# A Mamba block beside a recurrence: elementwise steps moved from VectorE to GpSimd, gate results kept in PSUM, and a new order of the pieces

## The chip, the core and the metric

The kernel runs on one core of a Trainium2 chip. The core has five engines that run their own instruction streams and wait for each other by semaphores: TensorE (PE, matmuls into PSUM), VectorE (DVE, elementwise and scans), ScalarE (ACT, activations), GpSimd (POOL[...]) and SyncE (SP, which issues most DMAs). The metric is device time in microseconds of one execution; lower is better. All numbers are float32.

## What is computed

The input is x with 8 samples of 512 tokens and 256 features. Four layers follow, each with a normalized input and a residual:

```python
x = x + mamba_block(layernorm(x))       # layer 1
x = x + recurrence(layernorm(x))        # layer 2
x = x + attention(layernorm(x))         # layer 3
x = x + recurrence(layernorm(x))        # layer 4, the weights of layer 2
```

The Mamba block, cut to what matters here:

```python
h = layernorm(x, ln1_g, ln1_b)
xi, z = split(rmsnorm(h, rms_w) @ in_proj_w)
xc = silu(causal_conv4(xi) + conv_b)
dbc = xc @ x_proj_w
delta = softplus(dbc[..., :64] @ dt_proj_w + dt_proj_b)
Bm, Cm = dbc[..., 64:80], dbc[..., 80:96]
# for each of 256 channels and 16 states, over the 512 tokens:
hs = exp(delta * A) * hs_before + delta * xc * Bm
y = sum_over_states(hs * Cm) + D_param * xc
h = h + (y * silu(z)) @ out_proj_w
x = x + h
x = x + relu(layernorm(x, ln2_g, ln2_b) @ ffn_w1 + ffn_b1) @ ffn_w2 + ffn_b2
```

The recurrence goes over the 8 samples one after the other, with the 512 tokens as its batch:

```python
f = sigmoid(xt @ wf.T + c @ uf.T + bf)
i = sigmoid(xt @ wi.T + c @ ui.T + bi)
g = tanh(xt @ wc.T + c @ uc.T + bc)
c = f * c + i * g
# the output of all samples: tanh(x @ wo.T + c_final @ uo.T + bo)
```

## The kernel before

The program has two halves. In the first, `mamba_and_recurrence` (L769) runs layer 1 and, one sample behind it, layer 2's recurrence. In the second, `attention` (L1158) runs layer 3 with layer 4's recurrence in its gaps. The functions of the recurrence (`recurrent_step`, L560) serve both halves; `d.keep` is true in the second alone.

The first half is software-pipelined over the samples. Block b runs the scan of sample b in 16 slots. A slot has one `scan`: two units of 8 channels by 16 states on 128 partitions (32 units in all), a `tensor_tensor_scan` over 512 tokens for each (L381) and then a multiplication by C for each (L385). C lies in PSUM (copied there by `take_c`, L299). For a scan, ScalarE makes the decay `da` in PSUM (L365, three banks), GpSimd makes the increments `bx` in SBUF (L372, three buffers, two units at a time), and SP loads the rows of delta and delta*xc, repeated over the states, from DRAM into pairs of buffers (`load_unit`, L348, three pairs each). TensorE sums over the states every second slot (`y`, L388).

Around the scan, each slot runs pieces of other samples. The order is written out by hand in `SLOTS` (L713), `LAST` for block 7 (L733) and `REST` behind it (L752); `FRONT` (L761) runs ahead of block 0. Each engine runs its instructions exactly in the order of these words. The letter says whose piece it is: e is sample b+2 and i is sample b+1 (both of `mamba_in`, L168), a and c are sample b, o is sample b-1 (`mamba_out`, L403), r is sample b-1 and q sample b-2 (both of the recurrence). A name that ends in an underscore is the ScalarE part that evicts the matmul of the same name. `da0`, `da1`, `bx` and `ld` prepare units some slots ahead.

The pieces that the change and the prediction touch:

- `affine` (L183): h times ln1_g plus ln1_b, two VectorE instructions over 128 x 1024. `outer` and `residual` (L196, L200): u is x normalized, plus h.
- `soft_exp`, `soft_rest`, `soft_ln`, `soft` (L301 to L317): softplus of a number v with e = exp(-|v|) and w = 1 + e as relu(v) + ln(w) - ((w - 1) - e), where the last bracket is the rounding remainder of w. `soft` also makes delta*xc, after which `store_dl` and `store_dx` write both to DRAM for the next block's loads.
- `conv0`, `conv1` (L238), three VectorE steps each that read the in-projection's PSUM bank.
- `gate0`, `gate1` (L408): y plus D*xc, then times silu(z).
- `tanh` and `update` (L597, L605): the sigmoids are computed as (1 + tanh)/2 and the state is kept doubled, so the new state is half of (1 + f)*c plus (1 + i)*g. The three activations are read from the matmuls' PSUM banks and written to three SBUF tiles; the three VectorE steps of `update` then run in SBUF.

PSUM has eight banks here: three for da, one for C, one for y, and three (tag `mm`, `cx.fill`) for all other matmul results of the first half.

Of the kernel before, what the change touches and what calls it, by code (L numbers as in the profile page):

```python
# [167 lines left out]
def mamba_in(cx, a, t, b):  # L168
# [132 lines left out]
    def soft_exp():  # L301

        t.w = cx.tok.tile([P, KC, L], F32, tag="h", name=f"w_{n}")
        nc.scalar.activation(t.e, t.e, AF.Exp, scale=-1.0)
        nc.scalar.activation(t.w, t.e, AF.Identity, bias=cx.one)

    def soft_rest():
        nc.vector.scalar_tensor_tensor(t.e, t.w, -1.0, t.e, ALU.add, ALU.subtract)
        nc.vector.tensor_sub(t.dl, t.dl, t.e)
# [250 lines left out]
def recurrent_step(cx, d, b, tok, tok_tag, ch, ch_tag):  # L560
# [36 lines left out]
    def tanh(g, m):  # L597
        if g == 0:
            t.act = [
                cx.tmp.tile([P, L], F32, tag=f"act_{what}", name=f"act_{what}{m}_{n}")  # L600
                for what, _ in GATES
            ]
        gate_tanh(cx, g, m, t.ps[g, m], t.act[g])

    def update(m):  # L605
        if m == 0:
            t.s = cx.state.tile([P, KC, L], F32, tag="c", name=f"c_{n}")
        f, i, g = t.act
        for what, by in ((f, d.s[:, m, :]), (i, g)):
            nc.vector.scalar_tensor_tensor(what, what, 1.0, by, ALU.add, ALU.mult)  # L610
# [124 lines left out]
q.g0 bx ld da0 q.g0_ scan o.gate1 da1
q.f1 o.proj1 o.proj0 bx da0 y scan da1 o.add_proj ld o.stats
scan da0 o.norm bx o.turn1 o.turn1_ q.i1 ld da1 o.turn0
y ld q.update0 bx o.turn0_ o.up0 da0 da1 q.f1_ scan
da0 q.i1_ ld o.up1 da1 o.up0_ bx scan
ld y da0 bx scan da1  # L740
da0 bx o.up5 ld da1 scan o.up1_
da0 ld da1 y bx scan
o.up2 bx o.up3 o.up2_ scan ld da0 o.up3_ o.down1 c.gate0 o.down0 o.up4 da1 o.add1
o.up6 ld o.up4_ o.up5_ o.up6_ da0 scan y bx da1 o.up7
da0 ld o.add0 bx o.up7_ scan da1
scan bx o.residual o.down3 o.down2 c.bias o.add3 o.add2 y da0 q.output0 r.stats r.norm q.g1 ld da1
# [677 lines left out]
```

## Time and profile before

| | us |
|---|---|
| median of three runs | 1674.97 (1673.49 to 1677.93) |
| the profiled execution | 1674.03 |
| its span in the trace | 1672.3 |
| PE busy | 1483.9 (89%) |
| DVE busy | 1206.1 (72%) |
| ACT busy | 869.4 (52%) |
| POOL busy | 443.8 (27%) |

The page of the profile divides the span into 40 slices of about 42 us and gives each engine's busy share in tenths, 9 being 90% or more:

```profile
PE   3146888989898989898879999999999999999998
DVE  4499999999999998982136677567675766665435
ACT  4565767576766666442223555454554445454522
POOL 1346464655555555553100000000000000000000
```

The first 18 slices or so are layer 1 with layer 2's recurrence; attention begins at about 860 us. In a view of groups, a row gives the line of the code and the engine, the operation, output and inputs with shapes, the count, then the busy time and the mean duration of one in ns, and then how long the engine was idle just before them and who ended the wait. In the timeline a row gives the start and duration in us, and in brackets the idle time before it. A PE matmul in float32 leaves two records.

### The profile page before, as it was taken

How to read it: one execution, taken by the hardware profiler on the slowest of the kernel's cores; microseconds unless marked ns; L12 is line 12 of the kernel's file. 1: busy time of each engine (PE TensorE's matmuls, PEld its weight loads, DVE VectorE, ACT ScalarE, POOL GpSimd, SP SyncE). 2: the span in 40 equal slices, each digit the busy share in tenths (PEclk: the TensorE clock that was granted, in tenths of full speed). 3: DMA queues.
4: the chain of work that ended last, by engine and by line, in shares of the span. 5: the costliest groups of instructions: out<-in, count | busy, mean ns of one | idle time of the engine just before them, and what ended most of it. 6: DMA issues, size and time to landing. Idle time of an engine off the chain costs nothing.

```text
span 1672.3 us, 19586 instructions
## 1 busy us (share of the span) xinstructions
PE 1483.9 (89%) x6756; PEld 697.5 (42%) x6756; DVE 1206.1 (72%) x1678; ACT 869.4 (52%) x1315; POOL 443.8 (27%) x271
## 2 busy tenths in 40 slices
PE   3146888989898989898879999999999999999998
PEld 1012545555464646464642333333333333333346
DVE  4499999999999998982136677567675766665435
ACT  4565767576766666442223555454554445454522
POOL 1346464655555555553100000000000000000000
PEclk9576999999999999999986999999999999999999
DMA  5799888888788888860210111111011110100023
GB/s 190 193 237 240 216 226 210 246 207 239 197 228 218 220 204 221 224 150 26 66 51 20 26 35 30 34 24 39 15 40 24 38 27 26 24 9 26 27 94 126
DMA packets 110404, 196.03 MB, mean 117 GB/s; under 512 B 16448, under 2 KB 25984, under 8 KB 110304
## 3 DMA queue, kind: packets, MB, share of 16 engines
q1 hardware_dynamic: 107648, 186.61, 42.3%
q10 hardware_dynamic: 1824, 5.15, 0.9%
q0 software_dynamic: 832, 3.02, 0.6%
q8 instruction: 53, 0.87, 0.2%
q14 instruction: 47, 0.39, 0.1%
HBM read 159.06 MB, written 23.07 MB: 109 GB/s over the span
## 4 chain that ended last, share of the span: by engine, by line
PE 61%; DVE 21%; ACT 9%; issue 3%; DMA 3%; POOL 1%; SPq 1%; ACTq 0%; DVEq 0%; POOLq 0%
PE ps_s_c L998 10%; PE ps_e_c L998 9%; DVE hc_a L381 8%; PE ps_o_c L1044 8%; DVE hc_a L385 3%; PE ps_f_o L491 2%; ACT da_a L365 2%; PE ps_f_o L467 2%; PE ps_v_c L972 2%; PE ps_w_c L1085 2%; PE ps_f_d L540 2%; PE ps_i_d L540 2%; PE ps_g_d L540 2%; PE ps_f_d L549 2%; PE ps_i_b L540 2%
## 5 line engine op out<-in xcount | busy, mean ns | idle before, releaser
L1009 DVE TENSOR_REDUCE mp<-ps_s_c 128x2 f32<-128x1024 f32 x256 | 301.8, 1221 | 186.6 <-PE ps_s_c L998 186.1
L372 POOL TENSOR_TENSOR bx_a<-dx_rep_a,B_a 128x1024 f32<-128x1024 f32 x128 | 302.6, 2369 | 280.2 <-DVE hc_a L381 234.2
L1035 ACT ACTIVATE e_c<-ps_e_c 128x1024 f32<-128x1024 f32 x256 | 248.9, 1021 | 158.7 <-PE ps_e_c L998 155.8
L381 DVE TENSOR_TENSOR_SCAN hc_a<-da_a,bx_a 128x512 f32<-128x512 f32 x256 | 300.0, 1209 | 34.7 <-ACT da_a L365 21.8
L365 ACT ACTIVATE da_a<-dl_rep_a,neg_a 128x512 f32<-128x512 f32 x256 | 171.4, 684 | 85.9 <-DVE hc_a L381 65.2
L998 PE MATMUL ps_s_c<-keys,q_c 32*128 32x512 f32 x1024 | 186.9, 656 | 1.6 <-ACT e_c L1035 1.1
L998 PE MATMUL ps_e_c<-q_c,keys 32*128 32x512 f32 x1024 | 170.6, 650 | 3.7 <-DVE mp L1009 3.7
L385 DVE TENSOR_TENSOR hc_a<-hc_a,Cp_a 128x512 f32<-128x512 f32 x256 | 161.2, 671 | 0.0
L1044 PE MATMUL ps_o_c<-e_c,va 128*32 128x512 f32 x1024 | 139.8, 612 | 0.4 <-ACT oT_c L1060 0.3
L467 PE MATMUL ps_f_o<-h_o,w 128*128 128x256 f32 x512 | 124.3, 391 | 13.6 <-ACT f_o L480 5.9
L467 PEld LDWEIGHTS ps_f_o<-h_o,w 128*128 128x128 f32 x512 | 94.8, 192 | 57.4 <-ACT f_o L480 20.1
L491 PE MATMUL ps_f_o<-w,f_o 128*128 128x256 f32 x512 | 114.0, 381 | 0.0
L394 PE MATMUL y_a<-hc_a,sum 128*32 128x512 f32 x512 | 87.2, 654 | 22.8 <-DVE hc_a L385 12.8
L491 PEld LDWEIGHTS ps_f_o<-w,f_o 128*128 128x128 f32 x512 | 96.3, 190 | 15.7 <-ACT f_o L480 2.9
L998 PEld LDWEIGHTS ps_s_c<-keys,q_c 32*128 32x128 f32 x1024 | 60.5, 188 | 100.2 <-issue 39.6
L82 POOL TENSOR_TENSOR rs_d<-ve_d,neg_half 128x4 f32<-128x4 f32 x8 | 8.1, 1016 | 342.2 <-DVE ve_d L81 342.2
L998 PEld LDWEIGHTS ps_e_c<-q_c,keys 32*128 32x128 f32 x1024 | 51.8, 186 | 102.0 <-issue 67.3
L82 POOL TENSOR_TENSOR rs_c<-ve_c,neg_half 128x4 f32<-128x4 f32 x8 | 8.1, 1014 | 300.6 <-DVE ve_c L81 300.6
L480 ACT ACTIVATE f_o<-ps_f_o,vecs 128x256 f32<-128x256 f32 x128 | 52.5, 469 | 39.7 <-PE ps_f_o L467 39.5
L117 PE MATMUL ps_hT_a<-ident,h_a 128*128 128x128 f32 x64 | 12.9, 323 | 67.2 <-ACT h_a L206 60.7
L223 PE MATMUL ps_in_a<-hT_a,w_in 128*128 128x512 f32 x128 | 61.3, 615 | 0.8
L1044 PEld LDWEIGHTS ps_o_c<-e_c,va 128*32 128x32 f32 x1024 | 20.5, 108 | 93.2 <-issue 83.4
(213 smaller groups left out, 2091.2 us busy)
## 6 DMA issues: line engine op xcount, KB each, us to landing
dx_rep_a<-dx_dram_a SPq DMA_DIRECT2D x256, 256.0 KB, 5.7
dl_rep_a<-dl_dram_a SPq DMA_DIRECT2D x256, 256.0 KB, 5.6
x<-in_x_dram SPq DMA_DIRECT2D x8, 512.0 KB, 8.8
dl_dram_a<-dl_a SPq DMA_DIRECT2D x8, 512.0 KB, 4.7
dx_dram_a<-dx_a SPq DMA_DIRECT2D x8, 512.0 KB, 3.1
pre_dram_b<-pre_b ACTq DMA_DIRECT2D x8, 512.0 KB, 6.0
pre_back<-pre_dram_b SPq DMA_DIRECT2D x8, 512.0 KB, 3.4
keys<-xT_c SPq DMA_DIRECT2D x128, 32.0 KB, 1.9
```

Of the source, the lines that this page charges most:

```text
L365: cx.nc.scalar.activation(t.da[u], t.dl_rep[u // 2][:, u % 2, :], AF.Exp, scale=a.A[:, u : u + 1])
L372: cx.nc.gpsimd.tensor_mul(t.bx[pair], t.dx_rep[pair], t.B.unsqueeze(1).to_broadcast([P, 2, L]))
L381: cx.nc.vector.tensor_tensor_scan(t.hc[u], t.da[u], t.bx[pair][:, u % 2, :], 0.0, ALU.mult, ALU.add)
L385: cx.nc.vector.tensor_mul(t.hc[u], t.hc[u], t.Cp)
L394: cx.nc.tensor.matmul(t.y[k][head(j), :], a.sum[:, r, :], t.hc[4 * quad + j], start=(r == 0), stop=(r == QR - 1),)
L467: nc.tensor.matmul(ps[:, m, :], a.w1[:, k, ts(m0 + m, P)], t.h2[:, k, ts(half, L // 2)], start=(k == 0), stop=(k == KC - 1),)
L491: nc.tensor.matmul(ps, t.f[:, m, ts(c % 2, P)], a.w2[:, m, :], start=(m == 0), stop=(m == FC - 1),)
L540: cx.nc.tensor.matmul(ps, cx.gw[:, g, k, ts(m, P)], xT[:, k, :], start=(k == 0), stop=False)
L998: cx.nc.tensor.matmul(ps[:, i, :], lhs[rows, :], rhs[rows, :], start=True, stop=True)
L1009: cx.nc.vector.tensor_reduce(c.mp[:, t, h : h + 2, DH], ps, AX.X, ALU.max, negate=True)
L1035: cx.nc.scalar.activation(e, ps, AF.Exp)
L1044: cx.nc.tensor.matmul(po[head(j), :], c.va[b % 2][:, t, g * HG + j, :], es[j // 2][:, j % 2, :], start=(t == 0), stop=(t == TC - 1),)
```

## The change

For samples 1 to 7 the affine, the first residual and the two instructions of the softplus remainder run on GpSimd instead of VectorE (`side`). So that the remainder is a plain subtraction, ScalarE subtracts 1 from w in an instruction of its own, and the logarithm adds it again as its bias. In the first half, the tanh of gates f and g is written back to its own PSUM bank; a new piece `hold` makes (1 + f)*c into an SBUF tile and frees f's bank, and (1 + i)*g is written over g in PSUM. `gate_out` writes y plus D*xc back to y's bank. In the second half (`d.keep`) the same instructions as before are issued. The order of the pieces is new in `SLOTS` and `LAST`; `outer` and `residual` run two samples ahead instead of one. `LAST` follows `SLOTS` without the pieces of e and i.

```diff
@@ -170,6 +170,8 @@
     nc, v = cx.nc, cx.v
     n = f"a{b}"
 
+    side = nc.gpsimd if b else nc.vector
+
     def stats():
         t.x = cx.X[b]
@@ -181,8 +183,8 @@
         normalize(cx, t.h, t.x, t.inner)
 
     def affine():
-        nc.vector.tensor_mul(t.h, t.h, cx.rows3["ln1_g"])
-        nc.vector.tensor_add(t.h, t.h, cx.rows3["ln1_b"])
+        side.tensor_mul(t.h, t.h, cx.rows3["ln1_g"])
+        side.tensor_add(t.h, t.h, cx.rows3["ln1_b"])
 
     def square():
         t.ms = cx.small.tile([P, TC], F32, tag="ms", name=f"ms_{n}")
@@ -199,7 +201,7 @@
 
     def residual():
 
-        nc.vector.tensor_add(t.u, t.u, t.h)
+        side.tensor_add(t.u, t.u, t.h)
 
     def scale():
         for c in range(TC):
@@ -303,13 +305,14 @@
         t.w = cx.tok.tile([P, KC, L], F32, tag="h", name=f"w_{n}")
         nc.scalar.activation(t.e, t.e, AF.Exp, scale=-1.0)
         nc.scalar.activation(t.w, t.e, AF.Identity, bias=cx.one)
+        nc.scalar.activation(t.w, t.w, AF.Identity, bias=cx.minus)
 
     def soft_rest():
-        nc.vector.scalar_tensor_tensor(t.e, t.w, -1.0, t.e, ALU.add, ALU.subtract)
-        nc.vector.tensor_sub(t.dl, t.dl, t.e)
+        side.tensor_sub(t.e, t.w, t.e)
+        side.tensor_sub(t.dl, t.dl, t.e)
 
     def soft_ln():
-        nc.scalar.activation(t.w, t.w, AF.Ln)
+        nc.scalar.activation(t.w, t.w, AF.Ln, bias=cx.one)
 
     def soft():
         nc.vector.tensor_add(t.dl, t.dl, t.w)
@@ -408,9 +411,9 @@
     def gate_out(k):
 
         nc.vector.scalar_tensor_tensor(
-            t.xc[:, k, :], t.xc[:, k, :], v["D"][:, k : k + 1], t.y[k], ALU.mult, ALU.add
-        )
-        nc.vector.tensor_mul(t.zs[:, k, :], t.zs[:, k, :], t.xc[:, k, :])
+            t.y[k], t.xc[:, k, :], v["D"][:, k : k + 1], t.y[k], ALU.mult, ALU.add
+        )
+        nc.vector.tensor_mul(t.zs[:, k, :], t.zs[:, k, :], t.y[k])
 
     def proj(i):
@@ -563,7 +566,7 @@
     nc = cx.nc
     n = f"{d.name}{b}"
     t = Ctx()
-    t.ps = {}
+    t.ps, t.act = {}, {}
 
     def stats():
         t.x = cx.X[b]
@@ -595,20 +598,33 @@
         state(g, m)
 
     def tanh(g, m):
-        if g == 0:
-            t.act = [
-                cx.tmp.tile([P, L], F32, tag=f"act_{what}", name=f"act_{what}{m}_{n}")
-                for what, _ in GATES
-            ]
-        gate_tanh(cx, g, m, t.ps[g, m], t.act[g])
+
+        ps = t.ps[g, m]
+        if GATES[g][0] == "i" or d.keep:
+            t.act[g] = act_tile(g, m)
+        else:
+            t.act[g] = ps
+        gate_tanh(cx, g, m, ps, t.act[g])
+
+    def act_tile(g, m):
+        what = f"act_{GATES[g][0]}"
+        return cx.tmp.tile([P, L], F32, tag=what, name=f"{what}{m}_{n}")
+
+    def hold(m):
+
+        f = t.act[0]
+        t.held = f if d.keep else act_tile(0, m)
+        nc.vector.scalar_tensor_tensor(t.held, f, 1.0, d.s[:, m, :], ALU.add, ALU.mult)
 
     def update(m):
         if m == 0:
             t.s = cx.state.tile([P, KC, L], F32, tag="c", name=f"c_{n}")
-        f, i, g = t.act
-        for what, by in ((f, d.s[:, m, :]), (i, g)):
-            nc.vector.scalar_tensor_tensor(what, what, 1.0, by, ALU.add, ALU.mult)
-        nc.vector.scalar_tensor_tensor(t.s[:, m, :], f, 0.5, i, ALU.mult, ALU.add)
+        if d.keep:
+            hold(m)
+        i, g = t.act[1], t.act[2]
+        new = i if d.keep else g
+        nc.vector.scalar_tensor_tensor(new, i, 1.0, g, ALU.add, ALU.mult)
+        nc.vector.scalar_tensor_tensor(t.s[:, m, :], t.held, 0.5, new, ALU.mult, ALU.add)
         if m == KC - 1:
             d.s = t.s
@@ -635,8 +651,8 @@
 
     pieces = {f.__name__: f for f in (stats, norm)}
     for name, f in (
-        ("turn{}", turn), ("turn{}_", turn_), ("update{}", update), ("output{}", output),
-        ("output{}_", output_),
+        ("turn{}", turn), ("turn{}_", turn_), ("hold{}", hold), ("update{}", update),
+        ("output{}", output), ("output{}_", output_),
     ):
         for i in range(2):
             pieces[name.format(i)] = lambda f=f, i=i: f(i)
@@ -711,42 +727,42 @@
 
 
 SLOTS = """
-y da0 da1 a.take_c bx scan ld
-q.g0 i.outer bx ld da0 q.g0_ scan o.gate1 da1 i.rms i.residual
-i.scale q.f1 o.proj1 o.proj0 i.turn0 bx i.turn0_ da0 y scan da1 o.add_proj ld i.turn1 i.turn1_ o.stats
-i.proj0 scan da0 i.proj0_ o.norm i.conv0 bx i.proj1 o.turn1 i.proj1_ o.turn1_ q.i1 ld da1 o.turn0
-y ld q.update0 bx o.turn0_ i.conv1 o.up0 da0 da1 q.f1_ scan
-da0 i.proj2 q.i1_ i.proj3 ld i.silu_x o.up1 i.silu_z i.xproj da1 o.up0_ bx scan
-ld y da0 i.xproj_ bx scan da1
-da0 i.dt0 i.dt1 bx o.up5 e.stats ld i.dt0_ da1 scan i.dt1_ o.up1_ i.soft_exp
-da0 ld da1 y bx scan
-o.up2 bx o.up3 o.up2_ scan i.rows ld i.soft_rest da0 o.up3_ o.down1 c.gate0 o.down0 o.up4 da1 o.add1 i.soft_ln
-o.up6 ld e.center o.up4_ i.soft e.affine o.up5_ i.store_dx o.up6_ da0 scan y bx da1 o.up7
-da0 ld o.add0 bx o.up7_ scan e.square da1
-scan bx o.residual o.down3 o.down2 c.bias o.add3 o.add2 y da0 q.output0 r.stats i.store_dl r.norm q.g1 ld da1
-da0 q.output0_ scan bx da1 q.g1_ q.output1 r.turn0 ld r.turn0_
-scan q.update1 y r.turn1 ld bx r.turn1_ r.f0 da0 da1
-r.i0 bx da0 r.f0_ scan da1 ld q.output1_ r.i0_
+da0 y a.take_c bx i.rms i.scale scan q.g0 o.gate1 i.turn1 i.turn0 ld q.i0_ q.g0_ i.turn1_ da1 i.turn0_
+da0 scan q.update0 da1 ld o.proj0 o.proj1 i.proj0 bx
+scan bx y o.add_proj ld da0 i.proj0_ o.stats da1
+bx i.proj1 ld da0 q.f1 scan o.norm o.turn0 da1 i.proj1_
+ld o.turn1 i.conv0 o.turn0_ y i.proj2 o.turn1_ q.f1_ i.proj3 i.conv1 da0 da1 i.silu_x scan o.up0 bx q.hold1
+i.xproj o.up3 i.silu_z bx o.residual ld da0 scan da1
+i.xproj_ y bx o.up0_ e.stats da0 ld i.dt1 scan da1
+bx i.dt1_ da0 o.up1 o.up1_ q.i1 o.up2 e.center ld scan i.rows da1
+q.i1_ ld da0 o.up2_ da1 y scan bx i.dt0
+da0 o.up3_ i.dt0_ i.soft_exp bx o.down1 da1 o.down0 scan o.add1 ld
+ld scan e.outer i.soft_rest da0 o.up4 i.soft_ln o.add0 c.gate0 o.up5 y bx o.up7 o.up4_ da1 o.up6 o.up5_ e.affine o.up6_
+i.soft o.up7_ da0 da1 scan bx i.store_dx q.output0 o.down3 o.down2 o.add3 ld
+e.square scan da0 o.add2 da1 ld bx y
+da0 r.stats q.output0_ q.g1 q.output1 q.g1_ r.norm i.store_dl scan r.turn0 c.bias r.turn0_ bx r.turn1 da1 ld
+r.turn1_ q.update1 r.f0 e.residual da0 q.output1_ y r.f0_ da1 ld scan bx
+ld scan da0 da1 r.hold0 bx r.i0
 """.strip().split("\n")
...
@@ -754,15 +770,15 @@
 o.turn0 o.turn0_ o.turn1 o.turn1_ o.up0 o.up0_ o.up1 o.up1_ o.up2 o.up2_ o.up3 o.up3_ o.down0
 o.down1 o.add0 o.up4 o.up4_ o.up5 o.up5_ o.add1 o.up6 o.up6_ o.up7 o.up7_ o.down2 o.down3 o.add2
 o.add3 r.stats r.norm r.turn0 r.turn0_ r.turn1 r.turn1_
-r.f0 r.f0_ r.i0 r.i0_ r.g0 r.g0_ r.update0
-r.f1 r.f1_ r.i1 r.i1_ r.output0 r.output0_ r.g1 r.g1_ r.update1 r.output1 r.output1_
+r.f0 r.f0_ r.hold0 r.i0 r.i0_ r.g0 r.g0_ r.update0
+r.f1 r.f1_ r.hold1 r.i1 r.i1_ r.output0 r.output0_ r.g1 r.g1_ r.update1 r.output1 r.output1_
 """.strip().split("\n")
 
 FRONT = """
 i.stats e.stats i.center i.affine i.square i.outer i.rms i.residual i.scale i.turn0 i.turn0_
-i.turn1 i.turn1_ i.proj0 i.proj0_ i.proj1 i.proj1_ i.conv0 i.conv1 e.center i.proj2 i.proj3
+i.turn1 i.turn1_ i.proj0 i.proj0_ i.proj1 i.proj1_ i.conv0 i.conv1 e.center e.outer i.proj2 i.proj3
 i.silu_z i.silu_x i.xproj i.xproj_ e.affine i.dt0 i.dt0_ i.dt1 i.dt1_ i.rows i.soft_exp i.soft_rest
-i.soft_ln i.soft i.store_dl i.store_dx e.square
+i.soft_ln i.soft i.store_dl i.store_dx e.square e.residual
 """
@@ -1254,6 +1270,8 @@
     make_identity(nc, cx.ident)
     cx.one = const.tile([P, 1], F32, name="one")
     nc.gpsimd.memset(cx.one, 1.0)
+    cx.minus = const.tile([P, 1], F32, name="minus")
+    nc.gpsimd.memset(cx.minus, -1.0)
     cx.neg_half = const.tile([P, 2 * TC], F32, name="neg_half")
     nc.gpsimd.memset(cx.neg_half, -0.5)
```

More of the change, by code (lines that the diff above doesn't have):

```diff
@@ L730 @@
+ld scan e.outer i.soft_rest da0 o.up4 i.soft_ln o.add0 c.gate0 o.up5 y bx o.up7 o.up4_ da1 o.up6 o.up5_ e.affine o.up6_
[4 more added lines that the diff above has]
+ld scan da0 da1 r.hold0 bx r.i0
 """.strip().split("\n")
 LAST = """
-y da0 da1 a.take_c bx scan ld
@@ L735 @@
[L735 to L746, printed above, removed]
@@ L747 @@
-da0 q.output0_ scan bx da1 q.g1_ q.output1 r.turn0 r.turn0_
-scan q.update1 y r.turn1 r.turn1_ r.f0 da0
-r.i0 r.f0_ scan q.output1_ r.i0_ r.g0 r.g0_ r.update0 r.f1 r.f1_ r.i1 r.i1_ r.output0 r.output0_ r.g1 r.g1_ r.update1 r.output1 r.output1_
+da0 y a.take_c bx scan q.g0 o.gate1 ld q.i0_ q.g0_ da1
+da0 scan q.update0 da1 ld o.proj0 o.proj1 bx
+scan bx y o.add_proj ld da0 o.stats da1
+bx ld da0 q.f1 scan o.norm o.turn0 da1
+ld o.turn1 o.turn0_ y o.turn1_ q.f1_ da0 da1 scan o.up0 bx q.hold1
+o.up3 bx o.residual ld da0 scan da1
@@ new lines @@
+y bx o.up0_ da0 ld scan da1
+bx da0 o.up1 o.up1_ q.i1 o.up2 ld scan da1
+q.i1_ ld da0 o.up2_ da1 y scan bx
+da0 o.up3_ bx o.down1 da1 o.down0 scan o.add1 ld
+ld scan da0 o.up4 o.add0 c.gate0 o.up5 y bx o.up7 o.up4_ da1 o.up6 o.up5_ o.up6_
+o.up7_ da0 da1 scan bx q.output0 o.down3 o.down2 o.add3 ld
+scan da0 o.add2 da1 ld bx y
+da0 r.stats q.output0_ q.g1 q.output1 q.g1_ r.norm scan r.turn0 c.bias r.turn0_ bx r.turn1 da1
+r.turn1_ q.update1 r.f0 da0 q.output1_ y r.f0_ scan
+scan r.hold0 r.i0 r.i0_ r.g0 r.g0_ r.update0 r.f1 r.f1_ r.hold1 r.i1 r.i1_ r.output0 r.output0_ r.g1 r.g1_ r.update1 r.output1 r.output1_
```

## Prediction

> **What bounds the kernel now.** I began with the page's slices: DVE stands at nine tenths in the first half alone, so only the first half (0 to about 850 us) is touched by a lighter VectorE. Next I cut that half by sample, from one take_c (L299) to the next: blocks 0 to 7 begin at 55.3, 146.1, 228.5, 319.4, 408.5, 499.1, 588.5 and 677.3 us. Windows over four of them:
>
> ```profile
> core 0: us, PE busy (x) PEld busy (x) DVE busy (x) ACT busy (x) POOL busy (x), PEclk, DMA share, GB/s
> 146.10:228.50 82.40, 67.12 (x259) 39.34 (x258) 80.49 (x121) 55.83 (x98) 48.60 (x27) 0.88 0.88 226
> 319.40:408.50 89.10, 81.52 (x321) 46.90 (x320) 85.84 (x126) 60.82 (x108) 48.51 (x27) 0.98 0.85 224
> 588.50:677.30 88.80, 81.52 (x321) 47.03 (x320) 82.04 (x114) 56.97 (x96) 46.57 (x24) 0.98 0.85 216
> 677.30:775.00 97.70, 91.17 (x348) 52.74 (x347) 76.02 (x107) 41.11 (x73) 39.32 (x20) 0.97 0.57 143
> ```
>
> Read: in a steady block VectorE works 85.8 of 89.1 us, GpSimd little over half. But the third line is a natural experiment. Block 6 prepares no sample two ahead, so VectorE has 4 us less to do than in block 5 (82.0 for 86.0), and the block is only 0.6 us shorter than block 5's 89.4. The chain of waits in block 6 lies on TensorE from 632 to 660 us. So TensorE is a second bound close behind the first; block 7 is TensorE's altogether.
>
> The groups by form, and three places of the timeline:
>
> ```profile
> L308 DVE SCALAR_TENSOR_TENSOR e_a<-w_a,e_a 128x1024 f32<-128x1024 f32 x8 | 18.3, 2282 | 9.9 <-ACT w_a L305 9.9
> L309 DVE TENSOR_TENSOR dl_a<-dl_a,e_a 128x1024 f32<-128x1024 f32 x8 | 9.8, 1225 | 0.3
> L372 POOL TENSOR_TENSOR bx_a<-dx_rep_a,B_a 128x1024 f32<-128x1024 f32 x128 | 302.6, 2369 | 280.2 <-DVE hc_a L381 234.2 <-DMA dx_rep_a<-dx_dram_a 45.8 <-DMA dl_rep_a<-dl_dram_a 0.2
> ...
> 460.17 2.36 POOL L372 TENSOR_TENSOR bx_a<-dx_rep_a,B_a 128x1024 f32<-128x1024 f32 x1 [2.88 <-DVE hc_a L381]
> 461.19 2.42 DVE L308 SCALAR_TENSOR_TENSOR e_a<-w_a,e_a 128x1024 f32<-128x1024 f32 x1
> ...
> 694.65 5.11 POOL L372 TENSOR_TENSOR bx_a<-dx_rep_a,B_a 128x1024 f32<-128x1024 f32 x2
> 696.60 0.96 DVE L610 SCALAR_TENSOR_TENSOR act_f_b<-act_f_b,c_b 128x512 f32<-128x512 f32 x1
> 697.48 2.83 DVE L610 SCALAR_TENSOR_TENSOR act_i_b<-act_i_b,act_g_b 128x512 f32<-128x512 f32 x1
> ...
> 431.05 0.63 PE L117 MATMUL ps_h_o<-ident,un_o 128*128 128x128 f32 x4 [2.19 <-DVE xc_a L241]
> 432.55 3.78 PE L540 MATMUL ps_i_b<-xT_b,gw 128*128 128x512 f32 x4 [0.87 <-ACT h_o L452]
> 436.12 3.12 PE L549 MATMUL ps_i_b<-c_b,gw 128*128 128x512 f32 x4
> ```
>
> At 461.19 an instruction that costs 1.23 us elsewhere ends 1.2 us after GpSimd's does: it waited. At 696.60 two GpSimd instructions stand back to back; VectorE's f update gets in between them, its i update then waits for the second (2.83 instead of 0.68), and the pair of GpSimd instructions takes 5.11 instead of 4.68. The two engines take turns. The last lines show a TensorE that ran dry for 3 us and then needs 6.9 us for eight records that take 3.76 elsewhere (1.88 for four at 753.13).
>
> [...]
>
> **The change, part by part, for a steady block.**
>
> 1. *VectorE loses.* Affine L184 and L185 2.44, residual L202 1.22, L308 with its wait 2.42, L309 1.22. The two f updates took 1.90 and 1.05 us in this block (401.84 and 430.82)[...]: the 0.69 of the undisturbed ones, so 1.57 less. The gated sum i*g, and the D term written to PSUM, change by under 0.1 each. Together 8.9: 86.0 becomes 77.1 us.
>
> 2. *GpSimd gains* five instructions of 2.36, 11.8 us: 48.5 becomes 60.3 of some 87. In throughput covered. Its FIFO matters: the softplus pair stands behind bx 11, the affine between bx 12 and 13. I followed the stream: bx 13 is ready about 5 us before its scan, so the scans are not starved.
>
> 3. *ScalarE gains* one 1024-wide Identity (w - 1), 1.15 as L305: 62 of 87, covered, except where it delays part 4.
>
> 4. *What becomes late: soft (dl + w, then dl * xc).* In the new order soft_exp, soft_rest, soft_ln and soft stand in slots 9, 10, 10, 11 (before: 7, 9, 9, 10). ScalarE can't pass the decay of unit 21 before scan 18 is done, since da has three banks. From that moment S, at issue pitch: da 0.58, up's Relu pair 0.72, dt pair 1.16, Exp 0.97, two Identity 2.1, da 0.58, e.outer 2.0, da 0.58, table load 1.28, Ln 1.06: S + 11.0. VectorE arrives after scan 19, two multiplies, an add, scans 20 and 21 with multiplies, an add and the gate: S + 8.0. A stall of 3.0. At S + 11.0 GpSimd is inside bx 12 (softplus pair from S + 5.6 to 10.3, bx 12 to 12.7): 1.6 more[...]. After the add GpSimd takes its turn with the first affine, 2.36, before the multiply gets in. So 7 us in all. Bounds: 0 if ScalarE runs ahead of my walk[...], 9.4 if both instructions meet a whole one; I take 7.
>
> 5. *TensorE.* The work is unchanged: up 14.6, down 14.0, y 8.0, in 7.0, x and dt 3.6, gates 20.6, outputs 3.6, out_proj 3.6, transposes 3.3, each from back-to-back stretches, 78.3 us. Before, it waits and runs slowly for 10.5 more. In the new order f1 fills the wait for o.norm, but f1 keeps one of three banks until hold1 at the end of slot 4. Both o transposes use one bank with a ScalarE copy between them (0.8), in2 waits for the second conv (about 1.6), up0 for hold1 (0.5), and xproj is queued behind up0. I find 4 to 5 us of waits, and 3 to 4 of half clock if the gap in slots 3 and 4 triggers it as at 432 us: 83 to 87. I take 86 to 87; nothing below 78.3, and above by rival D.
>
> 6. *Moved pieces and DMA queues.* store_dx still follows soft; store_dl goes from slot 12 to 13 and lies two loads ahead of the first dl load that reads it, so SP waits some 3.5 us there (landing 4.7 on the page). The loads are needed about 5 us later than they then land: hidden. At 0.85 DMA share a block of 87 needs 0.87; block 1's 0.88 fed a VectorE that was 98% busy: no bound.
>
> 7. *FRONT.* e.outer (2.06, four L108) now precedes the Silu on ScalarE, and the second Identity (1.15) precedes soft_rest; the chain runs through ScalarE's L108, L252, L255, L304 and L305 there. Nothing hides either: +3.2.
>
> 8. *Block 7 and the rest.* TensorE-bound. f1 ahead of the transposes covers part of the 4.7 us idle at 690: -2 (0 to -5). REST's last update loses one of three steps, 0.6. The attention half keeps its operations (d.keep): 0.
>
> VectorE then needs 77.1 + 7 + 1 to 2 of ScalarE waits = 85 to 86, TensorE 86 to 87. I take 87 for blocks 2 to 5 (mean now 90.0): 4 x 3.0 = 12.0. Block 6: 88.8 to 86.5, 2.3. Block 1 has no f updates of the recurrence: 7.3 saved, 6.3 lost to soft, 1.0. Block 0: DVE-bound from 86 us on, 6.1 saved, 6 lost, 0. Sum: 12.0 + 2.3 + 1.0 + 2.0 + 0.6 - 3.2 = 14.7. The profiled execution took 1674.03 (span 1672.3 and 1.7 around it), within 1 of the median 1674.97: 1674.0 - 14.7 = **1659**.
>
> **Rivals.** A is the above; with the period between 85 and 89 it spans 1648 to 1669.
>
> B: ScalarE and GpSimd are early, soft doesn't stall[...]. Both engines then meet near 82.5. For it: GpSimd idle for 40 of 89 us. Against: da's three banks keep ScalarE in step. Gains 7.5 x 4, 6.3, 4, 2.6, less 3.2: 1634.
>
> C: the gains of blocks just pay for FRONT: period 89, within 5 us of 1674.
>
> D, slower: the held banks. With one of three banks kept from f1 to hold1, and from g to its update, TensorE's queue stands behind a VectorE instruction at the end of a slot, runs dry[...]. It decides once TensorE's waits and slow stretches exceed 11.7 us a block (78.3 + 11.7 = 90.0; 10.5 now). At 92 a block: 2 x 4 + 3.2 + 1.0 + 3.2 lost = 15: 1689. For it: block 6 shows TensorE close to the bound, and slot 4 has these waits in a row. Against: slots 0 to 3 give it filler.
>
> **The numbers.** A 0.42, B 0.20, C 0.13, D 0.25. About 0.3% (5 us) is what a measurement here can tell from no change: faster is A and B, 0.62; same C, 0.13; slower D, 0.25. The range goes from B's time to D's, 1634 to 1690; A's own is 1648 to 1669.
>
> **What would show it.** Right: the groups of soft (dl, then dx, on VectorE) with waits on ScalarE's w and means well above 1.22; hold at 0.69; take_c 86 to 88 us apart; the first scan 3 us later. Wrong: soft at 1.22 without waits (B); take_c over 90 apart with TensorE waiting for act_f or c_b (D); scans waiting for bx, which would refute part 2.

## The result, and the profile after

The changed kernel takes 1666.2 us (median of six runs, 1661.0 to 1668.3) against 1673.6 (six runs, 1673.2 to 1677.9): ratio 0.9947, 95% interval 0.9931 to 0.9964. It is faster, by half a percent. The profiled execution took 1665.1 with a span of 1663.3, so 9.0 us are to be found between the traces. Cut at the `take_c` copies (L301 now), the gain and the loss stand apart:

| stretch | before | after | gain | predicted |
|---|---|---|---|---|
| FRONT | 55.3 | 58.9 | -3.6 | -3.2 |
| blocks 0 and 1 | 90.8 + 82.4 | 93.0 + 83.7 | -3.5 | +1.0 |
| blocks 2 to 5, mean of one | 90.0 | 86.8 | 4 x 3.2 | 4 x 3.0 |
| block 6 | 88.8 | 86.1 | +2.7 | +2.3 |
| block 7 and all behind it | 995.0 | 994.6 | +0.4 | +2.6 |

Windows of the changed kernel over blocks 0, 1 and 3 (length, then busy time and count of each engine, granted clock, DMA share, GB/s):

```profile
58.90:151.90 93.00, 41.46 (x93) 10.11 (x94) 71.39 (x89) 47.62 (x75) 59.64 (x28) 0.59 0.91 229
151.90:235.60 83.70, 69.08 (x261) 40.43 (x260) 78.47 (x116) 58.89 (x102) 60.84 (x32) 0.87 0.93 229
323.30:409.40 86.10, 81.77 (x321) 47.18 (x320) 80.64 (x123) 63.00 (x108) 61.01 (x32) 0.98 0.91 230
```

The third line, a steady block: GpSimd 61.0, TensorE as before at 81.8, and VectorE 80.6 where the sum had 77.1. The groups by form of VectorE in that block say where the 3.5 are:

```profile
L320 DVE TENSOR_TENSOR dx_a<-dl_a,xc_a 128x1024 f32<-128x1024 f32 x1 | 3.3, 3266 | 0.0
L318 DVE TENSOR_TENSOR dl_a<-dl_a,w_a 128x1024 f32<-128x1024 f32 x1 | 2.6, 2582 | 1.8 <-ACT w_a L315 1.8
L617 DVE SCALAR_TENSOR_TENSOR act_f_b<-ps_f_b,c_b 128x512 f32<-128x512 f32 x3 | 2.1, 685 | 0.0
L504 DVE TENSOR_TENSOR x<-x,ps_f_o 128x256 f32<-128x256 f32 x4 | 1.7, 418 | 3.2 <-PE ps_f_o L494 3.2
```

The two steps of `soft` cost 1.22 each without a neighbour; here they take 2.58 and 3.27, so 3.4 us are spent waiting inside them, and 1.8 more ahead of them for the logarithm. A third wait, 3.2 us for TensorE ahead of an x addition, was not in the forecast. The timeline of the next block shows the turn-taking:

```profile
464.65 2.36 POOL L312 TENSOR_TENSOR dl_a<-dl_a,e_a 128x1024 f32<-128x1024 f32 x1
466.60 1.15 ACT L315 ACTIVATE w_a<-w_a,one 128x1024 f32<-128x1024 f32 x1
466.97 2.37 POOL L375 TENSOR_TENSOR bx_a<-dx_rep_a,B_a 128x1024 f32<-128x1024 f32 x1
467.83 2.59 DVE L318 TENSOR_TENSOR dl_a<-dl_a,w_a 128x1024 f32<-128x1024 f32 x1 [1.84 <-ACT w_a L315]
469.30 3.34 POOL L186 TENSOR_TENSOR h_a<-h_a,rows 128x1024 f32<-128x1024 f32 x1
470.46 3.26 DVE L320 TENSOR_TENSOR dx_a<-dl_a,xc_a 128x1024 f32<-128x1024 f32 x1
472.72 3.21 POOL L187 TENSOR_TENSOR h_a<-h_a,rows 128x1024 f32<-128x1024 f32 x1
```

The addition waits until bx ends at 469.3, then GpSimd waits for it (3.34 instead of 2.36), then the multiplication waits for GpSimd. That is the sequence which part 4 of the forecast walked through. But does it cost time? The chain of waits through that block, in order of time (start, length, what):

```profile
432.12 0.64 PE ps_h_o L117 x4
...
434.73 1.87 PE y_a L397 x8
436.60 3.79 PE ps_in_a L225 x8
...
456.74 3.66 PE ps_f_o L494 x16
...
460.77 1.23 DVE hc_a L384
...
462.71 2.00 ACT u_a L108 x4
...
466.60 1.16 ACT w_a L315
...
467.83 2.60 DVE dl_a L318
...
470.46 3.26 DVE dx_a L320
```

Not shown are VectorE's pieces on both sides: from the `take_c` at 409.4 to 432.0 and from 473.7 to the next `take_c` at 495.3 the chain is VectorE without a wait. So a block is one run of VectorE (scans, updates, statistics, convolution), then one of TensorE from the transposes on, then the softplus with ScalarE's part ahead of it. The chain shows one route only. The experiments ask how far behind it the next one is.

### The profile page after: what moved, and what is told of

Read it like the earlier page. It is cut to its first block, busy times and chain, and to the rows that moved or that the text cites. A ratio compares the mean times of both kernels' runs of the same rounds, so it can differ in the third digit from the quotient of the medians.

```text
span 1663.3 us, 19592 instructions
## 1 busy us (share of the span) xinstructions
PE 1487.2 (89%) x6756; PEld 700.3 (42%) x6756; DVE 1169.9 (70%) x1643; ACT 884.3 (53%) x1323; POOL 529.9 (32%) x307
## 4 chain that ended last, share of the span: by engine, by line
PE 67%; DVE 19%; ACT 5%; DMA 4%; issue 3%; POOL 2%; SPq 1%; DVEq 0%; ACTq 0%; POOLq 0%
PE ps_s_c L1014 10%; PE ps_e_c L1014 9%; DVE hc_a L384 8%; PE ps_o_c L1060 8%; PE ps_f_o L470 5%; PE ps_f_o L494 4%; DVE hc_a L388 3%; PE ps_in_a L225 2%; PE ps_v_c L988 2%; PE ps_w_c L1101 2%; PE ps_f_d L543 2%; PE ps_i_d L543 2%; PE ps_g_d L543 2%; PE ps_f_d L552 2%; PE y_a L397 2%
## 5 line engine op out<-in xcount | busy, mean ns | idle before, releaser
L397 PE MATMUL y_a<-hc_a,sum 128*32 128x512 f32 x512 | 92.0, 699 | 23.9 <-DVE hc_a L388 15.5
L225 PE MATMUL ps_in_a<-hT_a,w_in 128*128 128x512 f32 x128 | 68.1, 671 | 1.1 <-ACT hT_a L220 1.1
```

The lines of the kernel that those rows point to most:

```text
L225: nc.tensor.matmul(ps, a.in_proj[:, k, ts(m, P)], t.hT[:, k, :], start=(k == 0), stop=(k == KC - 1))
L397: cx.nc.tensor.matmul(t.y[k][head(j), :], a.sum[:, r, :], t.hc[4 * quad + j], start=(r == 0), stop=(r == QR - 1),)
```

## The experiments

All were timed in five rounds with the kernel before beside them, but for the two on the order, in three. The ratio is to the kernel before on the same chip, and a difference in us below is one of two ratios times 1673.6. The last column is the mean of blocks 2 to 5 in the profiled execution, one for each kernel. How far such a single trace can be trusted is seen in FRONT: its words are the same in eight of these kernels, and it took from 58.8 to 60.7 us.

| run | median, us | ratio to before (95%) | block, us |
|---|---|---|---|
| before | 1673.6 | 1 | 90.0 |
| the change | 1666.2 | 0.9947 (0.9931 to 0.9964) | 86.8 |
| e1 outer late | 1664.1 | 0.9939 (0.9926 to 0.9953) | 86.9 |
| e2 affine away | 1661.3 | 0.9917 (0.9900 to 0.9935) | 86.8 |
| e3 all on VectorE | 1692.3 | 1.0105 (1.0088 to 1.0121) | 92.5 |
| e4 gates in SBUF | 1689.2 | 1.0096 (1.0079 to 1.0114) | 91.0 |
| e5 conv early | 1672.1 | 0.9996 (0.9987 to 1.0004) | 87.7 |
| e6 FRONT and rms | 1660.7 | 0.9930 (0.9918 to 0.9943) | 86.8 |
| e7 old order | 1723.9 | 1.0308 (1.0291 to 1.0325) | 97.0 |
| e8 order alone | 1710.9 | 1.0225 (1.0208 to 1.0242) | 96.3 |
| e9 conv and norm early | 1660.1 | 0.9916 (0.9900 to 0.9933) | 85.5 |
| e10 both | 1654.5 | 0.9890 (0.9874 to 0.9907) | 85.4 |
| e11 spare work in the slack | 1665.0 | 0.9939 (0.9926 to 0.9952) | 86.8 |
| e12 the same work in VectorE's run | 1688.4 | 1.0094 (1.0077 to 1.0110) | 89.7 |

The steady blocks come in two lengths. In the change blocks 3 and 4 take 86.0 us, blocks 2 and 5 take 87.5. The trace of the change shows one stretch in each in which TensorE's granted clock was 0.50, behind the transposes of the o sample: 3.4 us long in the former (433.5 to 436.9 in block 4) and 6.8 in the latter (519.0 to 525.8 in block 5). In e1, e2 and e11 two of the four blocks took 86.0 to 86.1 us and two 87.3 to 88.0, and e6 has the same mean, so these means can be compared.

### e1 and e2: relieve the softplus

```diff
-ld scan e.outer i.soft_rest da0 o.up4 i.soft_ln o.add0 c.gate0 o.up5 y bx o.up7 o.up4_ da1 o.up6 o.up5_ e.affine o.up6_
+ld scan i.soft_rest da0 o.up4 i.soft_ln o.add0 c.gate0 o.up5 y bx o.up7 o.up4_ da1 o.up6 o.up5_ e.affine o.up6_
...
-e.square scan da0 o.add2 da1 ld bx y
+e.square e.outer scan da0 o.add2 da1 ld bx y
```

> e.outer (four Identities of ScalarE, 2.00 to 2.06 us, between the softplus's Exp and its Ln) is moved two slots down, behind e.square. Theory SOFT (part 4 of the forecast: the late softplus delays VectorE, and VectorE's delay ends the block): the Ln ends 2.06 us earlier, VectorE's wait for it goes from 1.8 us to 0 in blocks 2 to 6 and from about 4.0 to 1.9 in blocks 0 and 1; 5 x 1.8 + 2 x 2.06 = 13 us less than the changed kernel, some 1653 us, steady blocks 84 to 84.5 us. Theory TENSORE (part 5: TensorE's queue with its waits and slow stretches sets some 86 us, the softplus's stall lies in its shade): within 2 us of 1666, with another wait of VectorE in the place of the one removed.

For e2 only `e.affine` moves, from the end of slot 10 to slot 9 behind bx:

```diff
-da0 o.up3_ i.dt0_ i.soft_exp bx o.down1 da1 o.down0 scan o.add1 ld
+da0 o.up3_ i.dt0_ i.soft_exp bx e.affine o.down1 da1 o.down0 scan o.add1 ld
```

> GpSimd's affine is moved from behind the softplus's remainder to slot 9, into GpSimd's idle 7 us before the remainder. Theory SOFT: the multiplication of dl and xc on VectorE falls from 3.26 us to about 1.2 since no GpSimd operation takes turns with it (that of dl and w keeps its 2.6 because of bx), 2.0 us a block in seven blocks, some 14 us less: 1652 us, and the wait for the Ln stays at 1.8. Theory TENSORE: within 2 us of 1666. If GpSimd is the limit in blocks 0 and 1 (bx late behind remainder and affine), these two shorten by more than the 2.0.

Neither shortened a steady block. In e2 the multiplication still took 3.26 us: with the affine gone, GpSimd's next instruction in the order of the words is a bx, which could take the turn; that it did was not shown. The expectation had overlooked that another instruction stands next in the queue. e2's median is some 5 us under the change's, and the intervals hardly overlap; but its trace shows equal blocks, and that execution, at 1664.9, was the slowest of its four. Whether the place of the affine is worth some us stays open. In e1 the wait for the logarithm did go, and a wait of 1.0 us for GpSimd's remainder (L312) came, with the addition at 3.37 instead of 2.58: 0.8 us saved by one, 0.8 lost by the other. So neither run made the softplus as a whole shorter. What e1 shows is the chain of its block 3, at the place where the softplus stood:

```profile
370.30 7.10 PE ps_f_o L494 x32
377.40 3.45 PE ps_f_o L470 x16
380.86 1.00 PE y_a L397 x8
381.85 3.65 PE ps_f_o L470 x16
385.50 1.73 PE ps_o_b L636 x8
387.23 3.47 PE ps_f_o L494 x16
390.72 0.04 DVE x L504
```

TensorE runs on without a gap through the whole of that stretch, and the x addition in slot 11 needs its result. It starts 67.85 us after `take_c` (322.87); in the changed kernel VectorE came through the softplus to the same addition at 477.17, 67.78 us after 409.39, and TensorE's 16th record for it ended at 477.13 in the same trace. The two routes are a tie within 0.1 us. The softplus's stall is real, but a shorter one could not have started this addition earlier as long as TensorE's run is as long as it is. That is read from the two traces; no run took the stall away.

### e11 and e12: the same spare work at two places

Six statistics instructions whose result nobody reads, ahead of the x addition in slot 9 (e11) or ahead of the scan in slot 13 (e12):

```diff
+    def spare():
+        st = cx.small.tile([P, 6], F32, tag="spare", bufs=1, name=f"spare_{n}")
+        for c in range(6):
+            nc.vector.bn_stats(st, t.x[:, c % TC, :])
...
-da0 o.up3_ i.dt0_ i.soft_exp bx o.down1 da1 o.down0 scan o.add1 ld
+da0 o.up3_ i.dt0_ i.soft_exp bx o.down1 da1 o.down0 scan i.spare o.add1 ld
```

> Six statistics operations (128x256, 0.41 us each, 2.5 us) of VectorE whose result nobody reads are added ahead of the first x addition in slot 9, where VectorE of the changed kernel waits 3.1 us for TensorE and 1.8 us for the Ln. HANDOVER: they fill slack that TensorE's run covers; blocks stay at 86 to 87, within 4 us of 1666. BUSY of VectorE (its 80.6 us plus waits set the block): 7 x 2.5 = 17 us more, 1683.

> The same six statistics operations of VectorE (2.5 us) at another place: in slot 13, ahead of a scan, inside VectorE's own run from the last x additions to the transposes. HANDOVER: all of it is on the path, 2.5 us a block in seven blocks, 17 us more than 1666: 1680 to 1686, steady blocks 88.5. BUSY of TensorE: within 3 us of 1666, as at the other place.

Block 3 of e11, the window and VectorE's waits in it (all waits, how many, the longest):

```profile
323.96:410.02 86.06, 81.76 (x321) 47.13 (x320) 83.00 (x128) 63.17 (x108) 60.94 (x32) 0.98 0.87 230
```

```profile
DVE dl_a L323 <- ACT w_a L320: 1.9, 1, 1.9
DVE x L509 <- PE ps_f_o L499: 0.6, 1, 0.6
```

VectorE has 2.4 us more to do, its wait for TensorE fell from 3.2 to 0.6, and the block is as long as before. In e12 the same work cost 24.6 us, 3.5 us a block for 2.6 us of instructions. The window of its block 3, one of the two longest (blocks 2, 4 and 5 took 88.9 to 89.4):

```profile
332.38:423.83 91.45, 85.62 (x321) 49.17 (x320) 83.26 (x128) 62.75 (x109) 61.43 (x32) 0.93 0.82 220
```

The wait for TensorE was 3.7 us. TensorE, kept waiting 2.4 us at the transposes of the r sample (2.6 for all of them, 0.3 in the change), got a clock of 0.93 in this block instead of 0.98: around these transposes it was 0.79 (406 to 420 us) and then 0.96 (420 to 434), where the change had 1.00 at the same place of its block 4 (482 to 498), and the input product of gate f behind them took 845 ns a record instead of 618. So VectorE's time counts in its own run, with TensorE's lost clock on top, and not at all in TensorE's.

### e3, e4, e7, e8: the parts of the change one by one

e3 undoes the move to GpSimd:

```diff
-    side = nc.gpsimd if b else nc.vector
+    side = nc.vector
```

> Affine, residual and the softplus's remainder go back to VectorE in all blocks (the remainder as two subtractions, the second Identity stays); gates in PSUM and the new order are kept. VectorE gets 5 x 1.22 = 6.1 us a block; it loses the turn-taking with GpSimd in the softplus (1.4 + 2.0 us) and, as the remainder now fills it, the wait for the Ln (1.8). SOFT: +6.1 - 5.2 = +0.9 us a block, 1666 + 6 = 1672 us. BUSY (VectorE's busy time alone counts, so that the move to GpSimd was worth all its 6.1 us): 7 x 6.1 = 43 us more, 1709. TENSORE: within 2 us of 1666. In blocks 0 and 1, if GpSimd is their limit, 1 to 3 us less each.

It cost 26.4 us, 5.7 a steady block: the forecast of SOFT (0.9) failed, and BUSY came closest though not for its reason, since VectorE's busy time rose by 5.0 only (85.6). The residual (2.48 with a turn) lies in VectorE's run. The two remainder steps (2.48 and 1.23) lie ahead of `gate0`, which TensorE's next y has to wait for, since y has one bank: a wait of 2.5 us of TensorE for zs (L416). A second new wait of about the same size stands ahead of the out-projection. The change has neither; together they are 4.9 us, in a block that is 5.7 longer:

```profile
PE y_a L397 <- DVE zs_a L416: 2.5, 1, 2.5
PE ps_op_o L424 <- DVE c_b L627: 2.4, 1, 2.4
```

The x additions waited 5.6 us for TensorE.

e4 undoes the PSUM placement of the gates:

```diff
-        if GATES[g][0] == "i" or d.keep:
-            t.act[g] = act_tile(g, m)
-        else:
-            t.act[g] = ps
-        gate_tanh(cx, g, m, ps, t.act[g])
+        t.act[g] = act_tile(g, m)
+        gate_tanh(cx, g, m, t.ps[g, m], t.act[g])
...
-        t.held = f if d.keep else act_tile(0, m)
+        t.held = f
...
-        new = i if d.keep else g
+        new = i
```

> Gates f and g and the gated sum go back to SBUF (the hold updates f in place), GpSimd's part and the new order are kept. [...]L617 goes from 0.69 to about 1.47 us as before the change, 2 x 0.78 = 1.6 us a block on VectorE, in seven blocks 11 us: 1677. Rival ORDER: in the new order the hold stands where GpSimd is between two operations, or VectorE's loss lies in TensorE's shade: within 2 us of 1666.

It cost 24.9 us. Groups of its block 3:

```profile
L623 DVE SCALAR_TENSOR_TENSOR c_b<-act_f_b,act_i_b 128x512 f32<-128x512 f32 x2 | 3.4, 1708 | 0.1
L613 DVE SCALAR_TENSOR_TENSOR act_f_b<-act_f_b,c_b 128x512 f32<-128x512 f32 x3 | 3.3, 1088 | 0.0
L622 DVE SCALAR_TENSOR_TENSOR act_i_b<-act_i_b,act_g_b 128x512 f32<-128x512 f32 x2 | 2.9, 1426 | 0.0
```

In the change the same seven instructions take 0.69 each. Here all three steps take turns with GpSimd, mostly with bx: 2 x 1.0 + 3 x 0.4 + 2 x 0.7 = 4.7 us more, most of it in VectorE's run, and the block is 4.2 longer. The expectation of 11 us was right in kind and had less than half the size: it counted f's step alone.

e8 is the kernel before with only the new `SLOTS`, `LAST` and `FRONT` (without the holds):

```diff
-y da0 da1 a.take_c bx scan ld
-q.g0 i.outer bx ld da0 q.g0_ scan o.gate1 da1 i.rms i.residual
...
+da0 y a.take_c bx i.rms i.scale scan q.g0 o.gate1 i.turn1 i.turn0 ld q.i0_ q.g0_ i.turn1_ da1 i.turn0_
+da0 scan q.update0 da1 ld o.proj0 o.proj1 i.proj0 bx
...
```

> The new slot order alone, on the kernel before: all on VectorE, gates in SBUF, one Identity. ADDITIVE (what taking back the GpSimd part and taking back the PSUM part cost, 26 and 23 us, are independent): 1666 + 26 + 23 - 9 for the Identity less = 1706 us, so that the order alone loses over 30 us. Rival OVERLAP (both cost the same slack[...]): 1680 to 1692. If the order is a gain of its own: under 1673.

ADDITIVE held: 1706 expected, 1710.9 measured. The new order alone is a loss of 2.25%. Its updates stand where GpSimd has two bx to do: the six instructions of a block take 9.8 us instead of 5.7, which is 4.1 us more in a block that is 6.3 longer. What makes up the rest was not followed. One update of block 4:

```profile
510.64 0.98 DVE L610 SCALAR_TENSOR_TENSOR act_f_b<-act_f_b,c_b 128x512 f32<-128x512 f32 x1
511.01 5.58 POOL L372 TENSOR_TENSOR bx_a<-dx_rep_a,B_a 128x1024 f32<-128x1024 f32 x2
511.54 2.84 DVE L610 SCALAR_TENSOR_TENSOR act_i_b<-act_i_b,act_g_b 128x512 f32<-128x512 f32 x1
514.42 2.71 DVE L611 SCALAR_TENSOR_TENSOR c_b<-act_f_b,act_i_b 128x512 f32<-128x512 f32 x1
```

e7 is the opposite: the changed engines and PSUM placement in the old `SLOTS`, `LAST` and `FRONT`, each hold put right behind the tanh of its f gate:

```diff
-da0 i.proj2 q.i1_ i.proj3 ld i.silu_x o.up1 i.silu_z i.xproj da1 o.up0_ bx scan
+da0 i.proj2 q.i1_ q.hold1 i.proj3 ld i.silu_x o.up1 i.silu_z i.xproj da1 o.up0_ bx scan
...
-r.i0 bx da0 r.f0_ scan da1 ld q.output1_ r.i0_
+r.i0 bx da0 r.f0_ scan da1 ld q.output1_ r.i0_ r.hold0
```

> The engines and PSUM placement of the changed kernel in the slot order of the kernel before (SLOTS, LAST and FRONT of before; each hold stands right behind its f gate's tanh). FREED (VectorE's freed 6 to 9 us a block are what counts, the order is a detail): steady blocks 85 to 88 us as in the changed kernel, 1660 to 1672. ORDER (TensorE's stops depend on the order; with the old one what VectorE gains turns up as its waits for TensorE): steady blocks stay at 89 to 92, 1673 or more.

A loss of 3.1%, far beyond the 89 to 92 us a block of ORDER. In a block of 98.6 us VectorE is busy for 77.9, just the 77 that the forecast had computed, and its longest waits are for ScalarE, not for TensorE as ORDER had it:

```profile
DVE hc_a L384 <- ACT da_a L368: 6.8, 3, 3.8
DVE act_f_b L617 <- ACT ps_f_b L558: 6.0, 3, 3.9
```

The freed time was all there and turned into waits. 6.0 us of them belong to the place that was chosen for the holds, so this isn't the best that the old order could do; how much better it could was not tried. The change is therefore one thing: each half of it loses (2.3 and 3.1%), both together win.

### e5 and e9: shorten TensorE's run

```diff
-bx i.proj1 ld da0 q.f1 scan o.norm o.turn0 da1 i.proj1_
-ld o.turn1 i.conv0 o.turn0_ y i.proj2 o.turn1_ q.f1_ i.proj3 i.conv1 da0 da1 i.silu_x scan o.up0 bx q.hold1
+bx i.proj1 ld da0 q.f1 i.conv0 scan o.norm o.turn0 da1 i.proj1_
+ld o.turn1 o.turn0_ y i.proj2 o.turn1_ q.f1_ i.proj3 i.conv1 da0 da1 i.silu_x scan o.up0 bx q.hold1
```

In e5 `o.norm` stays behind the scan, in e9 it goes ahead of da0 (`bx i.proj1 ld o.norm da0 q.f1 i.conv0 scan o.turn0`).

> The first half of the convolution (i.conv0, three operations of VectorE, 2.27 us) is moved from behind the next scan pair to ahead of it, so that its PSUM bank comes free before the TensorE transposes of the output half's input (o.turn0) need it. TENSORE (steady blocks are set by TensorE's work and its stops): TensorE's wait of 2.2 us for xc in front of the transposes goes, and the stretch behind it with a granted clock of 0.80 over two slices of 4.3 us (1.7 us) becomes shorter; 2 to 4 us a block in seven blocks, 14 to 28 less than 1666: 1638 to 1652. PAIR (the two engines hand over to each other, and what one gains there the other loses since the scan pair comes 2.3 us later): within 3 us of 1666.

> As the run with the early convolution, and o.norm (ScalarE's four Identities that write un_o, the source of the transposes) goes ahead of da0 in the same slot, so that it isn't queued behind a da that waits for VectorE's scan. HANDOVER (a block is one run of TensorE, from the transposes o.turn0 to the last down product, and one run of VectorE, from there through the next Cp copy to the transposes; each has slack only while the other runs): VectorE's run is shortened at its end by about 2.2 us (un_o about 429.7 in place of 430.2 to 432 on the changed kernel's clock), the scan pair delayed by 2.3 us falls into VectorE's slack of 4.9 us; blocks 83.5 to 85, some 10 to 15 us less than 1666: 1651 to 1656. BUSY (TensorE's own work of 82 us with its unavoidable stops is the limit): within 3 us of 1666.

e5 lost 8 us, worse than PAIR's "within 3": the conv's wait was gone, but ScalarE's decay in front of the norm waits for the scan that now came 2.3 us later, so the norm came later too, and TensorE stopped for it (1.5 us) and for the copy behind it (1.6). e9 gained 5.2 us. By the median that is no more than e2; what sets e9 apart is that its blocks are shorter in the trace. Its block 3:

```profile
324.28:409.45 85.17, 80.73 (x321) 46.54 (x320) 80.53 (x122) 62.72 (x108) 60.97 (x32) 1.00 0.89 232
```

The chain of waits of this block holds no piece of TensorE any more: it goes from VectorE to the dt eviction, the logarithm and the softplus:

```profile
380.86 1.16 ACT w_a L315
382.10 2.59 DVE dl_a L318
384.71 3.26 DVE dx_a L320
```

TensorE's clock is 1.00 over this block (0.98 in the change), though it stops no less than there: 4.3 us in the block, 2.5 at once, for 4.1 and 2.2. What went is the half clock behind the stop. Here are the window with the stop in the change (block 4) and the one in e9:

```profile
430.90:435.20 4.30, 2.21 (x12) 1.34 (x16) 4.20 (x6) 1.76 (x3) 1.43 (x1) 0.80 1.07 252
345.00:349.00 4.00, 1.46 (x15) 0.59 (x13) 3.65 (x6) 2.83 (x5) 2.36 (x1) 1.00 1.00 255
```

HANDOVER had the direction, with 1.3 us a block instead of 2 to 3, for behind TensorE's run the softplus's route became the longer one. That makes the test of e10.

### e6 and e10: outside the blocks, and all together

```diff
-i.turn1 i.turn1_ i.proj0 i.proj0_ i.proj1 i.proj1_ i.conv0 i.conv1 e.center e.outer i.proj2 i.proj3
+i.turn1 i.turn1_ i.proj0 i.proj0_ i.proj1 i.proj1_ i.conv0 i.conv1 e.center i.proj2 i.proj3
...
-i.soft_ln i.soft i.store_dl i.store_dx e.square e.residual
+i.soft_ln i.soft i.store_dl i.store_dx e.square e.outer e.residual
...
-da0 y a.take_c bx i.rms i.scale scan q.g0 o.gate1 i.turn1 i.turn0 ld q.i0_ q.g0_ i.turn1_ da1 i.turn0_
+da0 y a.take_c i.rms bx i.scale scan q.g0 o.gate1 i.turn1 i.turn0 ld q.i0_ q.g0_ i.turn1_ da1 i.turn0_
```

> Two edits outside the steady blocks. In FRONT, e.outer goes back from between center and the next projections to the end (behind e.square): if part 7 of the forecast is right, the first Cp copy comes 2.0 us earlier (58.9 to 56.9). In slot 0, i.rms goes ahead of bx, so that GpSimd's small power operation isn't queued behind a bx that waits for its first loads: block 0 loses ScalarE's 5.9 us wait in L208 and VectorE's 5.4 us wait for da, if those are on its path: 3 to 5 us of block 0's 93.0; steady blocks 0. Sum 5 to 7 less: 1659 to 1661. Rival LOADS: block 0's path is the chain of dl_rep and dx_rep loads, which begin after the last store of FRONT: 2.0 us in FRONT, none in block 0: 1664.

FRONT went from 58.9 to 56.5, and in e10, which has the same words, to 55.7; with e.outer in its middle it was never under 58.8. So 2 us or more of the 3.6 were e.outer. Block 0 gained 1.0, no more than FRONT scatters between traces: ScalarE's wait in L208 fell from 5.9 to 1.6 us, but its waits for the loads of dl grew from 13.8 to 23.7 us. For block 0 that is nearer to LOADS (nothing) than to the 3 to 5 us of the other, although the median of 1660.7 lies where the other had put it.

e10 has the edits of e9, e1, e2 and e6 together, and the first x addition of slot 9 behind the next scan (slot 10 then begins `ld scan o.add1 i.soft_rest da0`).

> Both runs shortened together: early convolution and o.norm (TensorE's run), affine away from the softplus, e.outer late and the first x addition behind the scan (VectorE's run), with the two edits of FRONT and slot 0. HANDOVER: with the convolution and norm early the chain through a block goes through the softplus, so what gave nothing alone now counts: Ln's wait and part of the turn-taking, 1.5 to 3 us a block below 85.2, and 3.5 us in FRONT and block 0: 1637 to 1650. Rival: the relief of the softplus gives nothing here either (GpSimd's remainder ends as late as the Ln, and bx takes turns in the affine's place), and only FRONT and block 0 count: 1655 to 1658.

1654.5 us, 1.1% under the kernel before and the fastest of all. But steady blocks are 85.4 as in e9, so the rival was right, within half a us: of the 9.5 us under the change 6.2 lie in blocks 2 to 6, which are as long as in e9, and 3.2 in FRONT (55.7). VectorE's waits in its block 3:

```profile
DVE x L504 <- PE ps_f_o L494: 1.8, 1, 1.8
DVE dl_a L318 <- POOL dl_a L312: 1.4, 1, 1.4
```

GpSimd's remainder is now what comes last before `soft`, and the chain is TensorE's run once more, with a granted clock of 0.98 over that block. Two routes of nearly the same length are left; a version that shortens the softplus itself (remainder and turns) and TensorE's run was not tried.

## Why the prediction was right, and where not

The forecast was 1659, 0.9% faster; measured 1666.2, 0.4% above it and within its range, in the likeliest case A. Of the gain of 14.7 us the traces show 9.0. The parts on VectorE's work, on the turn-taking and on TensorE's stops are right in kind; how they add up to a block was not, and that the block came out at 86.8 for 87 is in part luck (4 and 5).

1. VectorE's loss: right. 80.6 busy less the 3.4 of turn-taking is 77.2; 77.1 was computed. `hold` is at 0.685; that it would stay there with f in PSUM was the author's estimate, and this is the measured figure. What part 1 missed is seen in e4: in the new order not only f's step would wait for GpSimd but all three, 4.7 us a block and not 1.6. The PSUM placement is no extra of this change; its order needs it.
2. GpSimd: right, 61.0 for 60.3, and in steady blocks no scan waits for bx.
3. ScalarE's Identity: covered, as said.
4. The softplus is late: the walk is right instruction by instruction, the size 1.8 + 1.4 + 2.0 = 5.2 and not 7. The step that failed is adding those us to VectorE's path as if nothing else led there: TensorE's run ends within 0.1 us of it, as the traces of the change and of e1 show. What the sum lacked is the wait of 3.2 us for TensorE ahead of the x addition, in which e11's work cost nothing. The forecast added 7 and 1 to 2 to 77.1, the trace 5.2 and 3.2 to 77.2: two errors that nearly cancel. By the same tie, rival B (soft without a stall, 82.5 a block) would not have come true by a punctual softplus alone; that is argued, not run.
5. TensorE: right in kind. 4.1 us of waits (4 to 5); of half clock 1.7 us in blocks 3, 4 and 6 (in block 4 two slices of 4.3 us at 0.80) and 3.4 in blocks 2 and 5 (3 to 4 expected, after the stretch at 432 us of the kernel before, where the clock was 0.60 from 431 to 435 and 0.55 from 435 to 439); a period of 86.8 (86 to 87 taken, 87 in the sum). With the 78.3 of work that makes 84.1 or 85.8; the other 2 us are in stretches where its records are longer and weren't traced further.
6. Queues and DMA: no wait of steady blocks points there.
7. FRONT: 3.6 for 3.2. e.outer cost at least the 2.06 taken (e6, e10). For the second Identity less may be left than the 1.15 taken: without e.outer, e6 is 1.2 us over the kernel before, e10 0.4, and e7, with the old words and that Identity, 0.4.
8. Block 7 and the rest: 0.4 for 2.6. f1 covers just 0.7 of the 4.7 us (4.0 are left). A new wait of 2.2 us of the down product for f_o stands against it and against a wait of 1.8 for y that went.

The 5.7 us between 14.7 and 9.0: 4.5 lie in blocks 0 and 1, 2.2 in block 7, 0.4 in FRONT; blocks 2 to 6 gave 1.4 more than computed. Blocks 0 and 1 are the term with the wrong sign. There VectorE waits 4.0 and 3.9 us for the logarithm, twice the steady wait, and in block 1 VectorE's busy time fell by 2.0 (80.5 to 78.5) while its waits grew by 3.3. That these waits are on the path is argued from the trace; e6 moved block 0 by 1.0 and e1 by 1.3, and no run settled it. The order alone (e8) has 91.3 and 83.4 there, 1.5 of the 3.5 us, without any wait for the logarithm. e3, with GpSimd's part back on VectorE, has 94.0 and 85.2, so that part being on GpSimd is not shown to be what made them longer. The cause stays open.

Three slips of the working bear on nothing above. The upper bound of 9.4 us in part 4 does not follow from its terms: 3.0 and twice 2.36 are 7.7. The 10.5 us of TensorE's stops in part 5 and in rival D are those of block 6; the mean block had 90.0 less 78.3, 11.7 us, so D had no margin by its own sum. The instruction at 461.19 ends 1.1 us after GpSimd's, not 1.2.

Rival D was right to watch the banks, but decides in another kernel: the held bank stops TensorE for no time that the trace of the change shows, whereas in the old order (e7) holds that wait for tanh stop VectorE for 6.0 us.

## What to carry to other kernels

When two engines hand over to each other once in every iteration, busy time taken from one of them counts only inside its own run. Find the runs in the chain of waits and measure the slack by adding harmless work: the same 2.5 us cost nothing at one place and 3.5 us at another. And before crediting a saved stall, look for the second route to the same instruction; here it was 0.1 us behind.

An order written by hand fits one distribution of the work over engines and buffers: try a change of engines and its order together, since each alone can lose several times what both win.
